# Layer 3 of a four-layer convolution kernel: shifted copies replaced by 64x64 products that share the array with Layer 0's mixing

## The chip, the cores and the metric

The kernel runs on one core of one Trainium2 chip. The metric is the device time of one execution in microseconds; the time before is the median of three executions. One execution was also recorded by the hardware profiler, and all rows and waits below come from that record.

## The reference

The input is x of shape (16, 64, 128, 128): 16 images of 64 channels, float32. Four layers are added to it in turn, each on a group-normalized input `_gn` (32 groups of two channels):

```python
# layer 0: gram matrix of the channels, then a 64x64 matrix
y = einsum('bcd,bdn->bcn', einsum('bcn,bdn->bcd', xf, xf) / N, xf);  x = x + einsum('oc,bchw->bohw', conv_w, y)
# layer 1: 3x3 Scharr filters per channel
x = x + abs(conv(gn, kx)) + abs(conv(gn, ky))
# layer 2: quarter of the channels moved a column left, a quarter right, then a dense 3x3 convolution
x = x + conv3x3(shift(gn), W) + b
# layer 3: dense 3x3 convolution with weights -1, 0, 1, a 1x1 convolution, batch normalization, clip
y = conv1x1(conv3x3(gn, w_bin), w1x1) + b1x1
x = x + clip(leaky((y - mean) * rsqrt(var + EPS) * gamma + beta), 0, 255)
```

Layer 3's mean and variance run over all images, so its output can be finished only when all 16 images have passed its convolution.

## The kernel before, in words

**Staging.** Each image is cut into NS = 8 pieces of 8 rows per half image (128 partitions hold 64 channels twice). The loop at line 1059 runs over steps; in a step each stage works on one piece: `Front` (Layers 0 and 1) starts image b at step 15 + 8b, `Layer2` ten steps later, `Layer3` ten more (line 1009). So Layer 3 runs in steps 35 to 162, 128 pieces. `Front` mixes its last piece at step 140, `Layer2` ends at step 152, and Layer 3 is alone for the last ten steps. After that a last stage reads y and x3 back, applies the batch normalization and writes the output.

**Order.** Every instruction keeps its program order on its engine (`InOrder`, line 63). A step has four quarters, q = 0 to 3, and in each the stages come in the order Layer3, Layer2, Front (line 1067). What follows on an engine in a quarter is thus written out by hand.

**Layers 2 and 3 as products.** A pair of output rows shares work: `one` is the sum over the tap row that both need (`shared`, line 750), and `two` has the two rows' own parts, from row differences `d2` or `d3` that VectorE makes (`difference`, line 706). All products are 128 contracted rows by 64 output channels, issued two at a time, one for each half of the array's columns (`issue`, line 730; leftovers wait in `held` until `issue_rest` before Front in q = 1 and 3). Of the weights of `own` (line 753), one output half is dense, that is, it takes both input halves: three taps, three products. The other half is sparse: only one of the two 64-row input halves counts, so that a plain tap would use half of the array's rows:

```python
TO_PAIRS = [(0, 0, 0, 1), (0, 0, 1, 0), (0, 1, 0, 0), (1, 0, 1, 2), (1, 1, 0, 2), (1, 1, 1, 1)]   # n, input half, output half, ky
def single(table, n):        # the output half of n that is sparse, and its only input half
```

For n = 0 that is input half 0 to output half 1, for n = 1 input half 1 to output half 0. Before, two of the sparse half's three taps are packed into one product with full rows: `pk` holds both taps' weights, and a twin tile `qd` holds the difference and, in the other 64 partitions, a copy moved by a column. The third tap is a product of its own. So `own` has 3 + 2 products for each of n = 0, 1, and with the 3 + 3 of `shared` Layer 3 has 16 per piece, eight pairs; Layer 2 has the same 16.

**The twins.** Layer 2's are made by two DMAs on the GpSimd queue each (line 810). Layer 3's are made by ScalarE: `twin` at line 952 issues two copies of 64x512; `twin(0)` in q = 3, `twin(1)` in q = 0 of the next step (lines 999 and 963). `own(n=0)` of Layer 3 is issued in q = 0, `own(n=1)` in q = 1.

**Mixing.** Layer 0's product is `abd` (64x64 per half) times x. For the first three images it is issued as a pair of 128x64 products (`mix`, line 589). From image 3 on, `mix_four` (line 579) issues four 64x64 products in q = 1, one on each of the array's four 64x64 blocks. For that, `load` (line 564) lays x out so that one half of the partitions has the first four rows of the piece in both image halves, and the other half the last four: row block g then produces `po` of group g in both column blocks. Its outputs are two PSUM tiles, `po` and `g`, each with one buffer, which ScalarE reads into `xh`.

**Around them in a step.** VectorE makes the Scharr sums `u`, `e` (eight passes over 128x1024), then `y` = `two` + `c` for Layer 3 in q = 2 (line 990), `d3[0]` in q = 2 (line 996), `d3[1]` in q = 3 (line 1000), `d2[1]` at the end of q = 3, and `x3` and `d2[0]` in q = 0. ScalarE reads `po` into `xh`, normalizes, takes absolute values and squares, and copies `one` to `c`. In three steps out of eight, until about 1590 us, TensorE also has 42 or 44 gram products. At an image's end a chain of tiny operations (`coefficients`, line 288) crosses VectorE, TensorE and ScalarE; its first link, `s`, waits on VectorE for a square that ScalarE makes.

Of the kernel before, what the change touches and what calls it, by code (L numbers as in the profile page):

```python
# [10 lines left out]
F32 = mybir.dt.float32  # L11
# [5 lines left out]
P = 128  # L17
# [3 lines left out]
R = 8  # L21
NS = HH // R
EARLY = 3
CP = 4
# [84 lines left out]
def tile_kernel(ctx: ExitStack, tc: tile.TileContext, x, cw_h, w2_t, b2, wbin_t, w1_t, b1, gamma, beta, consts, out):  # L109
# [56 lines left out]
    def cols(o):  # L166
        return slice(o * C, (o + 1) * C)
# [51 lines left out]
    for name in ("d2", "d3"):  # L219
        diffs[name] = wpool.tile([P, 2, CP, W + 2], F32, name=name)  # L220
        pool.memset(diffs[name], 0.0)
        twins[name] = wpool.tile([P, 2, CP, W + 2], F32, name=f"q{name}")
        pool.memset(twins[name], 0.0)

    def weights_of_layer_3(ky):

# [11 lines left out]
    def other_weights():  # L238
        for n in range(2):
            o = 1 - single(TO_SLOTS, n)[0]  # L240
            pool.tensor_copy(wm[:, :, cols(o)], w2[:, n, :, cols(o)])

        for name, w, table in (("pk2", w2, TO_SLOTS), ("pk3", w3, TO_PAIRS)):
            dve.tensor_add(w[:, 2], w[:, 0], w[:, 1])
            packed[name] = wpool.tile([P, 2, C], F32, name=name)
            for n in range(2):
                o, i = single(table, n)
                for kx, half in ((1, i), (0, 1 - i)):
                    pool.tensor_copy(
                        packed[name][half * C:(half + 1) * C, n], w[i * C:(i + 1) * C, n, kx, o * C:(o + 1) * C]  # L250
                    )
# [297 lines left out]
    class Front:  # L549
# [14 lines left out]
        def load(self, i):  # L564
            b = self.b
            t = xin.tile([P, R, W], F32, tag="x", name=f"x_{b}_{i}")
            if self.four:

                t = t.rearrange("p (h r) w -> p h r w", h=2)
                v = x[b].rearrange("c (h r) w -> c h (r w)", h=2)  # L570
                for g in range(2):
                    j = (i * R + g * CP) * W
                    sp.dma_start(t[cols(g)].rearrange("p h r w -> p h (r w)"), v[:, :, j:j + CP * W])
            else:
                for h in range(2):
                    sp.dma_start(flat(t[h * C:(h + 1) * C]), halves(x[b].rearrange("c h w -> (c h w)"), h, i * R, R))
            self.xs[i] = t

        def mix_four(self, i):

            for g, (pool, tag) in enumerate(((ps_po, "po"), (ps_g, "g"))):
                self.po[i, g] = pool.tile([P, CP, W], F32, tag=tag, name=f"po_{self.b}_{i}_{g}")
            t = self.xs.pop(i)
            order = 1 - last[0], last[0]
            for g in range(2):
                for h in order:
                    pe.matmul(self.po[i, g][cols(h)], self.abd[cols(g), cols(g)], t[cols(g), h], start=True, stop=True)

        def mix(self, i, g):
            if self.b == 0 and (i, g) in ((0, 1), (1, 0)):  # L590
# [15 lines left out]
        def at(self, i, q):  # L606
            b = self.b
            if q == 0:
                if i == -3:

                    self.xe = xin.tile([P, W], F32, tag="xe", name=f"xe_{b}", bufs=1)
                    sp.dma_start(self.xe[lo], x[b][:, HH, :])
                    sp.dma_start(self.xe[hi], x[b][:, HH - 1, :])
                    sp.dma_start(x2_d[b][0:W].rearrange("(p w) -> p w", p=1), w0[0:1, 0:W])
                if i + 3 < NS and i + 3 not in self.xs:
                    self.load(i + 3)
                if -1 <= i < NS - 1:
                    self.prepare(i + 1, 1)
                if 1 <= i:
                    self.store(i - 1)  # L620
                    act.activation(
                        junk.rearrange("p (j w) -> p j w", w=W), self.x2.pop(i - 1), AF.Square,
                        accum_out=self.st[:, 1, i - 1:i],
                    )
                if i == NS:
                    chains.append(coefficients(self.st, lambda co: coefs2.update({b: co}), b2_sb))
            if q == 1 and -2 <= i < NS - 2:
                if i == -2:
                    self.abd, self.co = lead.pop(b)
                if i == -2 and not self.four:  # L630
                    self.pe = ps_g.tile([P, CP, W], F32, tag="g", name=f"pe_{b}")[:, 0, :]
                    small_product(self.pe, self.abd, self.xe)
                if self.four:
                    self.mix_four(i + 2)
                else:
                    self.mix(i + 2, 0)
            if q == 3 and i == -2 and self.four:
                self.pe = ps_po.tile([P, CP, W], F32, tag="po", name=f"pe_{b}")[:, 0, :]
                small_product(self.pe, self.abd, self.xe)
            if (i, q) == ((-1, 0) if self.four else (-2, 2)):  # L640
                nc.gpsimd.memset(self.chunk(0)[lo, 0, :], 0.0)
                self.normalized(self.chunk(0)[hi, 0, 1:1 + W], self.pe[hi], hi)
                self.pel = small.tile([P, W], F32, tag="pel", name=f"pel_{b}", bufs=1)
                self.normalized(self.pel[lo], self.pe[lo], lo)
            if q == 2:
                if i == NS - 2:
                    nc.gpsimd.memset(self.chunk(NS - 1)[hi, R + 1, :], 0.0)
                    act.copy(self.chunk(NS - 1)[lo, R + 1, 1:1 + W], self.pel[lo])
            if 0 <= i < NS:
                self.sobel(i, q)  # L650
            if q == 2 and -2 <= i < NS - 2:
                self.prepare(i + 2, 0)
            if q == 3 and -2 <= i < NS - 2 and not self.four:
                self.mix(i + 2, 1)
                self.xs.pop(i + 2)
# [85 lines left out]
    def issue_rest():  # L741
        while held[0] or held[1]:
            emit(1 - last[0] if held[1 - last[0]] else last[0])

    def products(p, wts, srcs):
        issue([taps(o, p, wts, srcs) for o in range(2)])

# [5 lines left out]
    def own(p, n, table, wt, name, m=CP, both=None):  # L753
# [7 lines left out]
        ]  # L761
        issue(some)


    tiles3 = {}

# [157 lines left out]
    class Layer3:  # L924
# [24 lines left out]
                norm(t[:, CP + 1:R, :], tiles[i][:, 1, 0:CP - 1], self.co)  # L949
                norm(t[:, R, :], tiles[i][:, 1, CP - 1, :], self.edge["upper"])  # L950

        def twin(self, n):

            d, q = diffs["d3"], twins["d3"]
            _, i = single(TO_PAIRS, n)
            act.copy(q[cols(i), n, :, 1:1 + W], d[cols(i), n, :, 1:1 + W])
            act.copy(q[cols(1 - i), n, :, 2:2 + W], d[cols(i), n, :, 1:1 + W])

        def at(self, i, q):
            b = self.b  # L960
            n = b * NS + i
            if q == 0 and 0 <= i < NS:
                self.twin(1)
                t = self.v[i]
                one = ps_one.tile([P, CP, W], F32, tag="one", name=f"one3_{b}_{i}")
                two = ps_two.tile([P, 2, CP, W], F32, tag="two", name=f"two3_{b}_{i}")
                self.p[i] = two, one
                shared(one, w3[:, 2], t)
                own(two[:, 0], 0, TO_PAIRS, w3, "d3")
            if q == 1:  # L970
                if 0 <= i < NS:
                    two, one = self.p[i]
                    own(two[:, 1], 1, TO_PAIRS, w3, "d3")
                    self.v.pop(i)
                    self.c = ring.tile([P, CP * W], F32, tag="c3", name=f"c3_{b}_{i}", bufs=1)
                    act.activation(self.c, flat(one), AF.Identity, bias=b1_sb)
                if i + 1 < NS:
                    self.prepare(i + 1)
                if 1 <= i:
                    y = self.y.pop(i - 1)  # L980
                    for s in range(2):
                        for z in range(2):
                            v = pairs(y_d[b], s)[:, (i - 1) * R:i * R, :].rearrange("c (n z) w -> c z n w", z=2)
                            sp.dma_start(v[:, z], y[s * C:(s + 1) * C, z])
# [11 lines left out]
                    difference("d3", 0, self.v[i + 1])  # L996
            if q == 3:
                if i + 1 < NS:
                    self.twin(0)
                    difference("d3", 1, self.v[i + 1])  # L1000
                if 0 <= i < NS:
                    act.activation(
                        junk, self.y[i].rearrange("p s j w -> p (s j w)"), AF.Square,
                        accum_out=bn_sq[:, n:n + 1],
                    )
# [53 lines left out]
    for step in range(starts[2][1] - 2, steps):  # L1059
        now[0] = step  # L1060
        for q in range(4):
# [5 lines left out]
            for stage, at in starts:  # L1067
                if stage is Front and q in (1, 3):
                    issue_rest()
                for b in range(B):  # L1070
                    run(stage, b, step - at - NS * b, q)
            if q in (0, 3):
                for b in range(B):
                    run(Layer2, b, step - starts[1][1] - NS * b, f"last of {q}")
# [116 lines left out]
```

## Time and profile before

| what | value |
|---|---|
| median of three executions | 2729.09 us (2726.27 to 2729.88) |
| span of the profiled execution | 2727.2 us, first to last instruction |
| TensorE, products | 2162.2 us busy, 79% of the span |
| VectorE | 2170.0 us busy, 80% |
| ScalarE | 2079.2 us busy, 76% |
| GpSimd | 852.7 us busy, 31% |
| ScalarE's copies into `qd` | 512, 315.4 us, 616 ns each |
| mixing products on 64x64 blocks | 832 records |
| last stage (from 2300 us) | DMA-bound: TensorE idle, 414 GB/s |

Each product of float32 is two records in the trace, one per pass; a pair of products is therefore four records. "us" in a timeline row is the time from the first start to the last end of the records merged in it, and the end of a product is modelled, so rows that follow each other overlap a little. Spacing is read from start to start. The number in brackets is the time for which the engine was idle before the row, with what ended it. The span lies 1.9 us under the median of the timed executions and inside their range; of the profiled execution no other time than its span is given.

### The profile page before, as it was taken

To read this page: it belongs to the slowest core of one execution; us is meant where nothing else is said; L and a number is where in the kernel's file an instruction comes from. 1 tells how busy PE (TensorE), PEld (TensorE's weight loads), DVE (VectorE), ACT (ScalarE), POOL (GpSimd) and SP (SyncE) were. 2 spreads that over 40 slices of the span, in tenths; PEclk is the share of its full clock that TensorE was granted. 3 is DMA by queue.
4 is the path that set the end of the run, shared out by engine and by line. 5 is a ranking of instruction groups with operands and counts; after the bars stand their busy time and mean duration, and the time that the engine had idled before them with its cause. 6 is when DMAs were issued, how large, how long until landed. Compare 5 with 4: busy or idle time off the path is not lost. (4 is left out here: it accounts for less than half of the span.)

```text
span 2727.2 us, 45742 instructions
## 1 busy us (share of the span) xinstructions
PE 2162.2 (79%) x14804; PEld 913.7 (34%) x14804; DVE 2170.0 (80%) x3495; ACT 2079.2 (76%) x3065; POOL 852.7 (31%) x1350
## 2 busy tenths in 40 slices
PE   6578899999999999999999999999999993000000
PEld 4234433434343434343434343333334641000000
DVE  4999999899999999999999999999995335333332
ACT  4766889898989898989898989899997667333332
POOL 2045424443434243333343334445453200000000
PEclk8689999999999999999999999999999996555555
DMA  8799878888888888888888887888877868999999
GB/s 199 205 239 239 226 197 239 225 235 225 235 228 237 227 226 229 226 227 234 225 224 237 214 204 203 207 211 216 224 200 186 226 188 314 420 420 420 420 420 385
DMA packets 693598, 685.93 MB, mean 252 GB/s; under 512 B 60096, under 2 KB 580448, under 8 KB 693360
## 3 DMA queue, kind: packets, MB, share of 16 engines
q1 hardware_dynamic: 668208, 613.83, 76.4%
q0 software_dynamic: 25152, 69.18, 10.0%
q8 instruction: 119, 1.95, 0.3%
q14 instruction: 119, 0.97, 0.1%
HBM read 346.23 MB, written 268.44 MB: 225 GB/s over the span
## 5 line engine op out<-in xcount | busy, mean ns | idle before, releaser
L73 PE MATMUL two<-d,w 128*64 128x508 f32 (+2 forms) x2560 | 848.9, 587 | 0.0
L73 PE MATMUL two<-d,wi 128*64 128x508 f32 (+3 forms) x1536 | 573.8, 577 | 0.0
L73 PE MATMUL two<-qd,pk 128*64 128x512 f32 (+1 forms) x1024 | 520.0, 589 | 24.5 <-DMA qd<-d 16.6
L73 POOL DMA_DIRECT2D qd<-d x512 | 271.1, 532 | 852.8 <-DVE d L73 323.9
L73 POOL TENSOR_SCALAR edges<-v,co 64x8 f32<-64x8 f32 x512 | 340.2, 664 | 349.0 <-ACT v L73 216.8
L73 DVE TENSOR_TENSOR d<-v 128x512 f32<-128x512 f32 (+1 forms) x512 | 346.6, 680 | 65.3 <-issue 37.5
L73 PEld LDWEIGHTS two<-d,w 128*64 128x64 f32 x2560 | 278.7, 136 | 320.0 <-issue 270.9
L73 PE MATMUL one<-v,w 128*64 128x508 f32 (+2 forms) x1600 | 364.3, 579 | 1.1 <-ACT v L73 1.1
L73 PE MATMUL one<-v,wi 128*64 128x508 f32 (+3 forms) x1536 | 353.3, 591 | 2.0 <-issue 1.4
L73 ACT COPY qd<-d 64x512 f32<-64x512 f32 x512 | 315.4, 616 | 19.9 <-DVE d L73 13.8
L73 DVE SCALAR_TENSOR_TENSOR e<-e 128x1032 f32<-128x1032 f32 (+1 forms) x256 | 313.0, 1223 | 0.0
L73 ACT ACTIVATE xh<-po,co 128x128 f32<-128x128 f32 (+1 forms) x480 | 275.9, 624 | 23.9 <-PE po L73 21.4
L73 PEld LDWEIGHTS two<-d,wi 128*64 128x64 f32 x1536 | 178.0, 135 | 197.4 <-issue 180.0
L73 DVE SCALAR_TENSOR_TENSOR y<-two,c 128x1024 f32<-128x1024 f32 x128 | 156.0, 1219 | 97.8 <-ACT v L73 45.6
L73 POOL TENSOR_SCALAR v<-v,kc 128x9 f32<-128x9 f32 x256 | 213.4, 847 | 12.0
L73 PE MATMUL po<-x,abd 64*64 64x512 f32 (+1 forms) x1024 | 177.1, 640 | 45.6 <-ACT xh L73 42.2
L73 ACT ACTIVATE v<-x,co 128x1024 f32<-128x1024 f32 (+3 forms) x256 | 203.8, 847 | 0.0
L73 ACT ACTIVATE u<-u 128x1024 f32<-128x1024 f32 x128 | 135.5, 1059 | 75.6 <-DVE u L73 74.6
L73 PEld LDWEIGHTS two<-qd,pk 128*64 128x64 f32 x1024 | 131.6, 135 | 176.9 <-issue 85.5
L73 PEld LDWEIGHTS one<-v,w 128*64 128x64 f32 x1600 | 130.9, 136 | 175.3 <-issue 146.5
L73 ACT ACTIVATE c<-one,co 128x512 f32<-128x512 f32 x128 | 86.7, 678 | 127.4 <-PE one L73 124.0
L73 DVE SCALAR_TENSOR_TENSOR u<-xh 128x1170 f32<-128x1170 f32 x128 | 175.4, 1370 | 4.2 <-ACT xh L73 4.1
(165 smaller groups left out, 3325.2 us busy)
## 6 DMA issues: line engine op xcount, KB each, us to landing
x<-in_x SPq DMA_DIRECT2D x256, 256.0 KB, 4.6
x_d<-u SPq DMA_DIRECT2D x512, 128.0 KB, 4.0
y_d<-y SPq DMA_DIRECT2D x512, 128.0 KB, 3.8
x_d<-x SPq DMA_DIRECT2D x496, 128.0 KB, 2.7
xr<-in_x SPq DMA_DIRECT2D x120, 512.0 KB, 5.9
qd<-d POOLq DMA_DIRECT2D x256, 130.0 KB, 3.3
qd<-d POOLq DMA_DIRECT2D x256, 129.8 KB, 3.8
v<-x_d SPq DMA_DIRECT2D x448, 72.1 KB, 3.0
```

What stands on the lines that cost most here:

```text
L73: return self.tc.keep_in_program_order(call(*args, **kwargs))
```

## The change

The shifted copies of Layer 3 go: `twin`, its two calls, the tile `qd3` and the packed weights `pk3`. `dense` issues the two dense halves of `two` together in q = 0: three taps for each half, six products of 128x64. `sparse` in q = 1 makes the three taps of each sparse half as 64x64 products on their own row and column block (row block 0 to column block 1, and row block 1 to column block 0), in a queue `blocks[0]`. `mix_four` no longer issues: it puts its four products, now each on row block h and column block h, in pairs in `blocks[1]`. `issue_blocks` takes one pair of each queue in turn: sparse, mixing, sparse, mixing, sparse. It is called from Front in q = 1 after `issue_rest`, and once more after the stages for steps without mixing. `load` is the same for all images now: 64 partitions by 4 KB in each of its two DMAs, where before a DMA of the later images had two runs of 2 KB for each partition.

```diff
-        twins[name] = wpool.tile([P, 2, CP, W + 2], F32, name=f"q{name}")
-        pool.memset(twins[name], 0.0)
+    twins["d2"] = wpool.tile([P, 2, CP, W + 2], F32, name="qd2")
+    pool.memset(twins["d2"], 0.0)
...
             dve.tensor_add(w[:, 2], w[:, 0], w[:, 1])
+            if name == "pk3":
+                continue
             packed[name] = wpool.tile([P, 2, C], F32, name=name)
...
-            if self.four:
-
-                t = t.rearrange("p (h r) w -> p h r w", h=2)
-                v = x[b].rearrange("c (h r) w -> c h (r w)", h=2)
-                for g in range(2):
-                    j = (i * R + g * CP) * W
-                    sp.dma_start(t[cols(g)].rearrange("p h r w -> p h (r w)"), v[:, :, j:j + CP * W])
-            else:
-                for h in range(2):
-                    sp.dma_start(flat(t[h * C:(h + 1) * C]), halves(x[b].rearrange("c h w -> (c h w)"), h, i * R, R))
+            for h in range(2):
+                sp.dma_start(flat(t[h * C:(h + 1) * C]), halves(x[b].rearrange("c h w -> (c h w)"), h, i * R, R))
...
-            order = 1 - last[0], last[0]
             for g in range(2):
-                for h in order:
-                    pe.matmul(self.po[i, g][cols(h)], self.abd[cols(g), cols(g)], t[cols(g), h], start=True, stop=True)
+                rows = slice(g * CP, (g + 1) * CP)
+                blocks[1].append([
+                    (self.po[i, g][cols(h)], self.abd[cols(h), cols(h)], t[cols(h), rows, :], True, True) for h in range(2)
+                ])
...
                 if self.four:
                     self.mix_four(i + 2)
+                    issue_blocks()
...
+    blocks = deque(), deque()
+
+    def issue_blocks():
+
+        while blocks[0] or blocks[1]:
+            for made in blocks:
+                for dst, wt, src, start, stop in (made.popleft() if made else ()):
+                    pe.matmul(dst, wt, src, start=start, stop=stop)
+        last[0] = 1
...
+    def dense(two, table, wt, name):
+
+        some = [None, None]
+        for n in range(2):
+            o, _ = single(table, n)
+            some[1 - o] = taps(1 - o, two[:, n], [wt[:, n]], [diffs[name][:, n]], 1)
+        issue(some)
+
+    def sparse(two, table, wt, name):
+
+        made = []
+        for n in range(2):
+            o, i = single(table, n)
+            made.append([
+                (dst, w[cols(i)], src[cols(i)]) for dst, w, src in taps(o, two[:, n], [wt[:, n]], [diffs[name][:, n]], 1)
+            ])
+        for m, both in enumerate(zip(*made)):
+            blocks[0].append([a + (m == 0, m == 2) for a in both])
...
-        def twin(self, n):
-
-            d, q = diffs["d3"], twins["d3"]
-            _, i = single(TO_PAIRS, n)
-            act.copy(q[cols(i), n, :, 1:1 + W], d[cols(i), n, :, 1:1 + W])
-            act.copy(q[cols(1 - i), n, :, 2:2 + W], d[cols(i), n, :, 1:1 + W])
-
...
             if q == 0 and 0 <= i < NS:
-                self.twin(1)
...
-                own(two[:, 0], 0, TO_PAIRS, w3, "d3")
+                dense(two, TO_PAIRS, w3, "d3")
...
-                    own(two[:, 1], 1, TO_PAIRS, w3, "d3")
+                    sparse(two, TO_PAIRS, w3, "d3")
...
                 if i + 1 < NS:
-                    self.twin(0)
                     difference("d3", 1, self.v[i + 1])
...
                 for b in range(B):
                     run(stage, b, step - at - NS * b, q)
+            issue_blocks()
```

## The prediction

> **What bounds the kernel now.** I read the page's busy times and groups first, then the table of busy time by stretch, then TensorE's timeline step by step, and last ScalarE's and VectorE's beside it.
>
> ```profile
> PE 2162.2 (79%) x14804; PEld 913.7 (34%) x14804; DVE 2170.0 (80%) x3495; ACT 2079.2 (76%) x3065; POOL 852.7 (31%) x1350
> L73 ACT COPY qd<-d 64x512 f32<-64x512 f32 x512 | 315.4, 616 | 19.9 <-DVE d L73 13.8
> ```
>
> Three engines look equally busy, and the change takes the copies' 315.4 us, the second row, from ScalarE. Whether that is worth anything depends on the stage (columns: stretch, length, then busy us of PE, PEld, DVE, ACT, POOL, clock, DMA):
>
> ```profile
> 600.00:2030.00 1430.00, 1417.60 (x9320) 558.89 (x9318) 1370.66 (x2229) 1291.88 (x1991) 570.96 (x909) 1.00 0.85 222
> 2030.00:2195.00 165.00, 165.00 (x839) 91.01 (x837) 85.48 (x155) 113.46 (x175) 56.14 (x115) 1.00 0.77 204
> 2195.00:2275.00 80.00, 77.89 (x351) 32.19 (x347) 25.14 (x51) 57.01 (x93) 0.00 (x0) 1.00 0.65 195
> ```
>
> While all stages run, TensorE is idle for 12.4 of 1430 us. Once mixing has ended (2030 to 2195) it is never idle. So only TensorE's own order and spacing count. A Layer 3 piece where nothing waits, and one that waits:
>
> ```profile
> 1253.66 2.73 PE L73 MATMUL one<-v,w 128*64 128x512 f32 x12
> ...
> 1260.60 1.09 PE L73 MATMUL po<-x,abd 64*64 64x512 f32 x8
> ```
>
> ```profile
> 1237.53 2.75 PE L73 MATMUL one<-v,w 128*64 128x512 f32 x12
> ...
> 1241.33 0.64 PE L73 MATMUL two<-qd,pk 128*64 128x512 f32 x1 [0.22 <-ACT qd L73]
> ...
> 1245.75 1.09 PE L73 MATMUL po<-x,abd 64*64 64x512 f32 x8
> ```
>
> From the first product of the piece to the mixing it is 6.94 us in one and 8.22 in the other. The bracket shows only 0.22: while one column half waits for its twin the other goes on, so that the engine counts as busy. ScalarE and VectorE in the slow piece:
>
> ```profile
> 1240.03 1.24 ACT L73 COPY qd<-d 64x512 f32<-64x512 f32 x2
> 1241.30 1.23 ACT L73 COPY xw<-xr 128x1024 f32<-128x1024 f32 x1
> 1242.54 1.25 ACT L73 COPY qd<-d 64x512 f32<-64x512 f32 x2
> ```
>
> ```profile
> 1213.43 0.17 DVE L73 TENSOR_REDUCE s<-st 128x2 f32<-128x16 f32 x1 [2.11 <-ACT junk L73]
> ...
> 1236.44 0.70 DVE L73 TENSOR_TENSOR d<-v 128x512 f32<-128x512 f32 x1
> ...
> 1238.29 0.68 DVE L73 TENSOR_TENSOR d<-v 128x512 f32<-128x512 f32 x1
> ```
>
> VectorE has both differences at 1238.97, in time for the 1240.09 at which the piece first needs one; ScalarE, late in its queue, has the twins at 1241.27 and 1243.79.
>
> **What the skill says.** The Trainium skill, TensorEngine Tiling (Array Packing), section Key Properties, says that changing the tiling mode, not just the tile, drains TensorE. The trace agrees. A step of Layers 2 and 3 without mixing:
>
> ```profile
> 2127.40 2.98 PE L73 MATMUL one<-v,w 128*64 128x512 f32 x12
> ...
> 2141.09 0.85 PE L73 MATMUL one<-v,w 128*64 128x512 f32 x2
> ```
>
> It is 13.69 us for 16 pairs, 0.855 a pair. A step with mixing and no wait is 14.85 (the `one` of Layer 3 begins at 1895.32 and again at 1910.17). The mixing thus costs 1.16: a slot of 0.855 and 0.31 for going to 64x64 blocks and back. I go by the 0.31. The same page, Gotcha 1: PSUM Pressure, says that different row tiles cannot use one PSUM bank at once. Before, each row block of the mixing has a bank of its own; after, both write the same one, in different partitions. No row shows that case; it is a rival below.
>
> **The change part by part.**
>
> *Slots in a full step.* Before: Layer 2 has 8 slots, Layer 3 has 8, the mixing 1, and one trip to 64x64 blocks. After: Layer 2 has 8, Layer 3's `shared` 3, `dense` 3, and the block phase 3, with the four mixing products inside its first two slots; one trip. 17 slots and 0.31 both times: 14.85. For all 104 pieces with four-block mixing (13 images of 8) the product time is unchanged. Bounds for the new kind of slot: in the mixing the two passes start 0.480 apart, against 0.427 within a run of pairs, but so do the first two after the return (0.484), so I take 0.427 for later passes; 0.480 for all is the upper end. Nothing in the trace points below 0.427, since a pass streams the same 512 columns.
>
> *Pieces without mixing.* 24 pieces: steps 35 and 36 (image 2 still mixes in pairs), 141 to 152 with Layer 2, 153 to 162 alone. Each pays a slot and a trip: 1.16. For the first 14, TensorE is the bound: +16.3. Alone, a piece now takes 7.82 and waits for ScalarE, because the twins stand between `d3` and the products:
>
> ```profile
> 2228.04 1.22 DVE L73 SCALAR_TENSOR_TENSOR y<-two,c 128x1024 f32<-128x1024 f32 x1 [5.38 <-issue]
> 2229.19 0.08 DVE L73 DVE_READ_ACCUMULATOR y<-two,c 128x1 f32 x1
> 2229.19 1.29 DVE L73 TENSOR_TENSOR d<-v 128x512 f32<-128x512 f32 x2
> ```
>
> After, 9 slots and the trip are 8.0. Another loop is as long: the end of `sparse`, `y` and both differences (2.44), `dense` (2.56), `sparse` with its drain (3.0), about 8.1. So 0.3 for each of ten: +3.
>
> *Waits on Layer 3's twins.* They go. I took the time from the piece's first product to the mixing, less 6.93, for each piece from 415 to 2016 us: two late pieces per image, 1.2 us each in the middle images, less in the last three, 21.5 us in all. What is late next? `dense` needs `d3[1]` 2.56 after the piece begins; in all these pieces it ends at 2.11 or earlier. TensorE would then come earlier to Layer 2, whose `d2[0]` twins are DMAs and land about 4.9 us after VectorE's difference; it already waits 11 us for them in all. VectorE does not wait for TensorE there, so these waits would absorb the gain if VectorE stayed where it is. It does not: at an image's end `s` waits 2.11 for a square that ScalarE makes behind two twins; without them ScalarE comes about 1.4 earlier, and VectorE keeps that until the gram steps. I let 2 of 21.5 come back: -19.5.
>
> *At nothing.* The mixing is issued two slots earlier and its second pair needs `g` read by ScalarE: that ends at 7.41 in the slow piece, 4.9 without 2.5 us of twins, and is needed at about 6. `y` on VectorE, and behind it `d3[0]`, comes after `sparse`, 1.2 later than after `own`; in steps with gram products VectorE has that room, elsewhere it is 2 to 5 us behind. If that cover is gone, VectorE's 14.33 us of work a step sets the pace, still under 14.85. x arrives a step ahead, and its two DMAs on SP stay two, of the same 256 KB. GpSimd loses a memset and four small copies early, and SP nothing; no DMA of Layer 3 was on their queues.
>
> *Sum* against the profiled span of 2727.2: -19.5 + 16.3 + 3 = -0.2. The median stands 1.9 above that span, so 2729.
>
> **The rivals.**
> 1. Slower: passes on the blocks stay 0.480 apart, since four weights are loaded for each. Four more passes (six, less the two already counted) times 128 pieces times 0.053: +27, 2756. It decides the sign from 0.01 us a pass. For: the mixing's row. Against: the pair after the trip starts just so, and the eight loads of the mixing lie within 0.21 us.
> 2. Slower: the waits return at `d2[0]`'s DMA, because VectorE is as late as before. Only 5 of 21.5 are won: +14, 2743. For: the 11 us. Against: the wait of `s`.
> 3. Faster: the earlier VectorE also takes away those 11 us: 2718.
> 4. The change doesn't do what it says: the four blocks do not run side by side, because of the shared bank. Then the mixing is four products in a row against three slots, 0.85 times 104: +89, 2818. The mixing's old form ran four at once, but with two banks.
>
> **How the numbers follow.** Forecast 0.36 (2723.6 to 2734.5, that is, within the 0.2% which a measurement of this kernel can tell from no change), rival 1 0.20, rival 2 0.20, rival 3 0.20, rival 4 0.04. Faster is rival 3; slower is rivals 1, 2 and 4. The range goes from rival 3 with both waits fully gone (-32.5 + 19.3, 2716) to just past rival 1, 2758; rival 4 is left out.
>
> **What would show it.** Steps without mixing at 14.85 instead of 13.68 and the last pieces near 8.1; passes in the block phase 0.427 apart, four starting within 0.03 us (rivals 1 and 4); Layer 3 pieces all near 8.0 from first product to Layer 2's; waits of `two` on the `qd` DMA at 8 to 12 us (rivals 2 and 3); ScalarE 315 us less busy; `s` waiting under 1 us. The forecast is wrong if the waits at `d2[0]` grow as Layer 3's vanish, or if a block slot is not 0.855.

## The result and the profile after

| | median, us | range | runs |
|---|---|---|---|
| before | 2729.5 | 2726.3 to 2730.9 | 4 |
| after | 2741.8 | 2738.6 to 2745.2 | 4 |

The ratio is 1.0049, 95% interval 1.0035 to 1.0063: slower by more than 0.2%, where no change was forecast. The profiled run of after took 2738.6, the lowest of its four; its span is 2736.8, against 2727.2 before. So the medians differ by 12.3 and the two traced spans by 9.6; the account below is of the 9.6. The granted clock is 1.00 in both from 600 to 2030 us.

The page of after, lines of engines and groups:

```profile
PE 2167.4 (79%) x15316; PEld 865.4 (32%) x15316; DVE 2169.2 (79%) x3495; ACT 1769.4 (65%) x2553; POOL 927.1 (34%) x1345
...
L73 PE MATMUL two<-qd,pk 128*64 128x512 f32 (+1 forms) x512 | 257.1, 583 | 26.3 <-DMA qd<-d 26.3
```

ScalarE is 310 us less busy and TensorE 5 us busier. The second row is now Layer 2's alone. What TensorE waited for in the stretch in which all stages run, first before, then after (columns: us in total, times, longest):

```profile
PE two L73 <- DMA qd<-d: 8.3, 12, 1.3
PE two L73 <- ACT qd L73: 7.0, 13, 0.7
```

```profile
PE two L73 <- DMA qd<-d: 17.6, 13, 2.8
PE one L73 <- issue: 1.7, 2, 1.4
```

The wait for ScalarE has gone; the one for `d2[0]`'s twin DMA has doubled, in about as many places. Most of it (15.8 of after's 17.6 us) lies at an image's end, in the step of Layer 3's last piece of that image, called the late step from here on. TensorE's timeline of after, in one late step:

```profile
1216.88 2.73 PE L73 MATMUL one<-v,w 128*64 128x512 f32 x12
1219.44 3.31 PE L73 MATMUL two<-d,w 128*64 128x512 f32 x14
1222.12 0.65 PE L73 MATMUL po<-x,abd 64*64 64x512 f32 x2
1222.59 0.59 PE L73 MATMUL two<-d,w 64*64 64x512 f32 x2
1222.60 0.60 PE L73 MATMUL po<-x,abd 64*64 64x512 f32 x2
1223.02 0.59 PE L73 MATMUL two<-d,w 64*64 64x508 f32 x2
...
1224.82 2.80 PE L73 MATMUL one<-v,wi 128*64 128x512 f32 x12
...
1231.52 0.61 PE L73 MATMUL two<-qd,pk 128*64 128x512 f32 x1 [1.34 <-DMA qd<-d]
```

Layer 3's piece takes 7.94 us (1216.88 to 1224.82), with no wait in it. Two mixing and two sparse products start within 0.02 us of each other, later passes 0.43 apart, though both row blocks of the mixing write one bank. Then, in Layer 2, TensorE stops for the twin.

A step with neither mixing nor waits, and two of the last pieces, from the same timeline:

```profile
2110.77 2.73 PE L73 MATMUL one<-v,w 128*64 128x512 f32 x12
2113.33 5.44 PE L73 MATMUL two<-d,w 128*64 128x512 f32 x24
...
2125.60 2.73 PE L73 MATMUL one<-v,w 128*64 128x512 f32 x12
...
2225.13 2.78 PE L73 MATMUL one<-v,w 128*64 128x512 f32 x12
2233.21 2.78 PE L73 MATMUL one<-v,w 128*64 128x512 f32 x12
```

The first takes 14.83 us where it was 13.69, the last piece 8.08 where it was 7.82. For the account I took each of the 128 pieces of Layer 3 from its first product to Layer 2's first (L3), and from there to the next piece (L2). Sums in us:

| | before | after | difference |
|---|---|---|---|
| start of the first piece | 312.5 | 309.6 | -2.9 |
| steps 35 and 36, L3 and L2 | 39.4 | 41.8 | +2.4 |
| 104 pieces with four-block mixing, L3 | 935.3 | 912.2 | -23.1 |
| the same, L2 | 743.7 | 757.2 | +13.5 |
| 12 steps without mixing, L3 and L2 | 165.4 | 179.5 | +14.1 |
| nine intervals of Layer 3 alone | 70.5 | 73.4 | +2.9 |
| TensorE's last product to the end | 448.8 | 451.8 | +2.9 |

With the last piece (0.1 shorter) and rounding this is the +9.6 of the spans. The start lies anywhere from 310 to 318 in the versions below, most of which do nothing there. The last row is 448.8 to 449.6 in every version whose last ten pieces have the old form; with the new form it is 451.3 to 451.8 in six and 449.0 to 450.7 in three, and what decides it was not found.

Row four is the one that the forecast had at +2. Nearly all of it (13.4) stands in the 13 late steps, 7.6 in two of them, at 429.7 and 692.2 us. And 13.0 stand in the nine late steps of the images beside which xr, the copy of x for a later image's gram, is still fetched; in the four after that, L2 of the late steps is 29.8 us before and 30.2 after.

### The profile page after: what moved, and what is told of

It is laid out like the page before. It is cut to its first block, busy times and chain, and to the rows that moved or that the text cites. A ratio compares the mean times of both kernels' runs of the same rounds, so it can differ in the third digit from the quotient of the medians.

```text
span 2736.8 us, 46307 instructions
## 1 busy us (share of the span) xinstructions
PE 2167.4 (79%) x15316; PEld 865.4 (32%) x15316; DVE 2169.2 (79%) x3495; ACT 1769.4 (65%) x2553; POOL 927.1 (34%) x1345
## 4 chain that ended last, share of the span: by engine, by line
PE 69%; DMA 19%; DVE 5%; issue 2%; SPq 2%; ACT 1%; POOL 0%; DVEq 0%; POOLq 0%; ACTq 0%
PE two L73 41%; PE one L73 22%; PE bank L73 4%; DMA qd<-d 2%; DVE u L73 2%; DMA end_x<-x_d 2%; DMA out<-end_x 2%; SPq L73 2%; DVE e L73 2%; DMA end_x<-y_d 1%; DMA out<-xw 1%; DMA xw<-x_d 1%; DMA xw<-y_d 1%; PE pg L73 1%; DMA v<-x_d 1%
## 5 line engine op out<-in xcount | busy, mean ns | idle before, releaser
L73 PE MATMUL two<-d,w 128*64 128x508 f32 (+4 forms) x3584 | 958.5, 590 | 0.0
L73 PE MATMUL two<-d,wi 128*64 128x508 f32 (+3 forms) x1536 | 575.7, 580 | 0.0
L73 POOL DMA_DIRECT2D qd<-d x512 | 271.0, 531 | 899.3 <-DVE d L73 368.1
L73 POOL TENSOR_SCALAR edges<-v,co 64x8 f32<-64x8 f32 x512 | 414.4, 809 | 229.2 <-ACT v L73 144.2
L73 PEld LDWEIGHTS two<-d,w 128*64 128x64 f32 (+1 forms) x3584 | 292.8, 134 | 514.5 <-issue 493.6
L73 DVE TENSOR_TENSOR d<-v 128x512 f32<-128x512 f32 (+1 forms) x512 | 346.9, 680 | 73.2 <-issue 45.7
L73 PE MATMUL one<-v,w 128*64 128x508 f32 (+2 forms) x1600 | 361.1, 579 | 0.0
L73 PE MATMUL one<-v,wi 128*64 128x508 f32 (+3 forms) x1536 | 349.1, 588 | 2.1 <-issue 1.7
L73 DVE SCALAR_TENSOR_TENSOR e<-e 128x1032 f32<-128x1032 f32 (+1 forms) x256 | 313.1, 1223 | 0.0
L73 PE MATMUL po<-x,abd 64*64 64x512 f32 (+1 forms) x1024 | 265.0, 629 | 46.6 <-ACT xh L73 43.6
L73 ACT ACTIVATE xh<-po,co 128x128 f32<-128x128 f32 (+1 forms) x480 | 275.5, 625 | 26.1 <-PE po L73 19.7
L73 PE MATMUL two<-qd,pk 128*64 128x512 f32 (+1 forms) x512 | 257.1, 583 | 26.3 <-DMA qd<-d 26.3
L73 ACT ACTIVATE u<-u 128x1024 f32<-128x1024 f32 x128 | 135.7, 1060 | 206.3 <-DVE u L73 206.2
L73 DVE SCALAR_TENSOR_TENSOR y<-two,c 128x1024 f32<-128x1024 f32 x128 | 156.0, 1219 | 114.3 <-issue 99.9
L73 PEld LDWEIGHTS two<-d,wi 128*64 128x64 f32 x1536 | 176.9, 136 | 205.1 <-issue 189.8
L73 POOL TENSOR_SCALAR v<-v,kc 128x9 f32<-128x9 f32 x256 | 216.8, 860 | 12.0
L73 ACT ACTIVATE v<-x,co 128x1024 f32<-128x1024 f32 (+3 forms) x256 | 203.9, 847 | 0.0
L73 ACT ACTIVATE c<-one,co 128x512 f32<-128x512 f32 x128 | 86.7, 677 | 159.7 <-PE one L73 155.1
L73 PEld LDWEIGHTS one<-v,w 128*64 128x64 f32 x1600 | 122.9, 137 | 183.2 <-issue 171.8
L73 ACT ACTIVATE v<-v,co 128x1154 f32<-128x1154 f32 x128 | 172.2, 1345 | 11.0 <-DMA v<-x_d 6.3
L73 DVE SCALAR_TENSOR_TENSOR u<-xh 128x1170 f32<-128x1170 f32 x128 | 175.4, 1370 | 3.9 <-ACT xh L73 3.8
L73 DVE SCALAR_TENSOR_TENSOR u<-xh,co,u 128x1024 f32<-128x1024 f32 x128 | 163.7, 1279 | 1.1 <-ACT u L73 1.1
```

The costliest lines, as they stand in the source:

```text
L73: return self.tc.keep_in_program_order(call(*args, **kwargs))
```

## The experiments

Theories on row four: A, x now goes in 4-KB packets, which hold up the twins; B, it is what stands ahead of the twins on the DMA queues at that moment; C, the twins cannot land earlier whatever is done. Unless said otherwise an edit is made on after, and waits are those of `two` on the `qd` DMA, 400 to 2040 us. Ratios are to the kernel before, with their 95% intervals. The code shown is the main part of each edit.

**1. The old form where nothing mixes.** In 24 pieces (`n < 2 or n >= 106`):

```
+                if n < 2 or n >= 106:
+                    own(two[:, 0], 0, TO_PAIRS, w3, "d3")
+                else:
                     dense(two, TO_PAIRS, w3, "d3")
```

and likewise for `sparse` and the copies.

> After, but the 24 pieces of Layer 3 beside which nothing mixes on four blocks keep the old form: the shifted copies on ScalarE and 2.5 slots each way instead of dense and sparse. If a piece without mixing pays a slot and a trip (1.16 us, 14 times) and 0.3 us in each of the last ten, the 12 steps without mixing go back from 14.84 to 13.68, the last pieces from 8.08 to 7.8, and the time falls by 16 to 19, to 2723 to 2726, under both kernels. If the added 12.3 us of the change lie elsewhere (other waits take over in these steps), it falls by under 8.

Measured: 2716.2, ratio 0.9944 (0.9933 to 0.9956). The steps without mixing in its timeline:

```profile
2085.87 2.98 PE L73 MATMUL one<-v,w 128*64 128x512 f32 x12
2099.55 2.98 PE L73 MATMUL one<-v,w 128*64 128x512 f32 x12
```

13.68 again, and 70.5 for the last nine intervals. The rows for these 24 pieces and the last row give 2.3 + 14.0 + 2.9 + 2.4 = 21.6 back, of 23.4 between the two spans. L2 of the 104 pieces, which this edit doesn't touch, is 6.3 shorter (750.9), and the start is 4.0 later. In the six late steps from 820 to 1480 us xr is issued 2.4 to 5.4 us ahead of the twins here and 1.5 to 4.1 in after; experiment 6 shows what that means. So the time falls by more than the 16 to 19 expected, but the price of an empty slot and a trip stands.

**2. The load of ScalarE alone.** The four copies are still made, but nothing reads them:

```
+                self.twin(1)
                 t = self.v[i]
...
+                    self.twin(0)
                     difference("d3", 1, self.v[i + 1])
```

> After, but ScalarE still makes the four shifted copies of every piece of Layer 3, into a buffer that no product reads: the change's products with the old load of ScalarE. If the earlier VectorE (s waits 0.67 in place of 2.11) is worth something after the change, it is lost here: d2[0] ends at 9.4 us in the late steps again, TensorE waits up to 1.3 us more in each image, and the time rises by 10 to 18, to 2752 to 2760. If the moment of d2[0] on VectorE does not matter because its twins land late whatever it does, the time stays within 4 us of 2742. In no case do TensorE's waits for Layer 3's twins come back.

Measured: 2748.5, ratio 1.0064 (1.0052 to 1.0076), +6.7 over after: between the two expectations. VectorE is as late as the first says; its `s` and `d2[0]` in the late step:

```profile
1217.34 0.17 DVE L73 TENSOR_REDUCE s<-st 128x2 f32<-128x16 f32 x1 [2.05 <-ACT junk L73]
...
1234.03 0.69 DVE L73 TENSOR_TENSOR d<-v 128x512 f32<-128x512 f32 x1
```

That is 2.05 against after's 0.67, and `d2[0]` ends 9.46 after the step begins (1225.26) against 8.07. The 104 pieces take 927.3 (L3) and 749.8 (L2), in sum 1677.1; before had 1679.0, after 1669.4. So 7.7 of the 9.6 that the 104 pieces win are lost again when ScalarE's queue is as long as before, though TensorE is free of the twins: Layer 3's mixing then waits for ScalarE instead (`[0.26 <-ACT xh L73]` ahead of the second pair, in the piece at 1225.26).

**3. The packets of x.** First with two fetches of 128 partitions, then with the same two fetches as after and a gap in the tile:

```
+                v = x[b].rearrange("c (h r) w -> h c r w", h=2)
+                for g in range(2):
+                    rows = slice(i * R + g * CP, i * R + (g + 1) * CP)
+                    sp.dma_start(flat(t[:, g * CP:(g + 1) * CP]), v[:, :, rows, :].rearrange("h c r w -> h c (r w)"))
```

```
+                t = xin.tile([P, 2, CP * W + 4], F32, tag="x", name=f"x_{b}_{i}")
...
+                    sp.dma_start(t[cols(h), :, 0:CP * W], v.rearrange("c (g n) -> c g n", g=2))
```

> After, but x of an image with four-block mixing is fetched in two DMAs of 128 partitions by 2 KB in place of two of 64 partitions by 4 KB; same bytes, same place on SP. Theory A (the twins of d2[0] land late because the 4-KB packets of x stand ahead of them on the DMA engines): TensorE's waits of two on the qd DMA fall from 17.6 us to 8 or less between 400 and 2040 us, and the time falls by about 10 to 15, to 2727 to 2733. Theory B (it is the moment at which SP issues x, 0.4 to 1.5 us ahead of the twins where it was 3.3 us before): the waits stay within 2 us of 17.6 and the time stays within 4 of the changed kernel's 2742. Theory C (the twin cannot land before a fixed moment of SP's saturated queue): as B.

> After, but the tile of x has a gap of 16 bytes between its two column groups, so that the same two fetches of 64 partitions go in packets of 2 KB (two per partition) instead of 4 KB; everything else as after. In the earlier try at this, x took 13.6 us to land, because its fetch had an outer dimension of 2; here the outer dimension is 64 as in the two kernels. Theory A (4-KB packets of x hold up the twins of d2[0]): TensorE's waits of two on the qd DMA fall from 17.6 us to 8 or less between 400 and 2040 us, time 2727 to 2733. Theory B (the moment of x on SP): waits within 3 us of 17.6, time within 4 of 2742.

Measured: the first took 3561.0 (ratio 1.304): no test of A, since the fetch itself became slow (last section). The second took 2740.8 (1.0043, 1.0030 to 1.0056), with waits of 18.6 us. A is false.

**4. x elsewhere.** Issued one quarter later; by ScalarE; or two quarters earlier (the old place is closed where the place is new):

```
+            if q == 1 and self.four and i + 3 < NS:
+                self.load(i + 3)
```

```
+            eng = act if self.four else sp
             for h in range(2):
-                sp.dma_start(
+                eng.dma_start(
```

```
+            if q == 2 and self.four and i + 4 < NS:
+                self.load(i + 4)
```

> After, but x for a later step is issued on SP one quarter later, behind Layer 3's stores and Layer 2's load of that quarter, so that it no longer stands just ahead of the twins of d2[0]; it still has more than half a step until the mixing reads it. Theory B (the moment of x on the queues): TensorE's waits of two on the qd DMA fall from 17.6 to under 9 us and the time by 8 to 15. Theory A (the size of its packets): about the same, since those packets are out of the way too. Theory C (the twins cannot land earlier whatever is ahead of them): waits of 16 to 19 us and no change in time. New waits of po for x would show that the later place is too late.

> After, but the two fetches of x per step of an image with four-block mixing are issued by ScalarE instead of SP. SP's queue, which is without a gap around the late steps, gets two issues a step shorter, so everything behind x on it comes 1.2 to 2.8 us earlier, and x stands elsewhere among the transfers. Theory B (moment of x): waits of two on the qd DMA fall to under 9 us, time 2727 to 2735. Theory C (the twin cannot land earlier): 2738 to 2745. ScalarE's two issues cost it at most 1.2 us a step, of the 2.5 that the change has taken from it; if that is felt, s waits over 1 us again.

> After, but x is issued on SP two quarters earlier, behind the stores of x3 of the step before (its buffer has been free since that step's mixing), so that it is neither next to xr nor just ahead of the twins of d2[0] in the steps after an image's end. Theory B (x and xr, 768 KB, go ahead of the twins on the same DMA engines): waits of two on the qd DMA fall from 17.6 to 4 to 9 us, without the waits for x that the later place brought, and the time falls to 2727 to 2734. If xr alone is enough to hold the twins, waits stay above 12 and the time above 2737.

Measured: later 2757.9 (1.0096), by ScalarE 2770.6 (1.0149), earlier 2741.1 (1.0037). The waits of the later place:

```profile
PE po L73 <- DMA x<-in_x: 9.0, 15, 1.9
PE two L73 <- DMA qd<-d: 4.2, 5, 1.7
```

The twins come in time more often, but x doesn't: L3 of the 104 pieces grows from 912.2 to 943.7. This speaks for B, but weakly, since TensorE is also later.

By ScalarE, the waits stay (15.5), where B expected under 9, and ScalarE waits 158.4 us for Layer 2's v, which was 3.7; why v comes late was not followed up. Yet in the ten late steps that still wait, the twins are used 3.6 to 4.4 us after their issue, sooner than in after (5.9 to 6.0 in four middle images). They wait because the twins are issued 9.5 to 11.0 us after the step begins, which was 8.6 in the middle images of after. So this run is no evidence against B.

The earlier place changed nothing (waits 17.7), but it was no test: between the old place of x in these steps and the new one lies only xr. x and xr had changed places and stayed neighbours.

**5. The twin earlier.** `d2[0]` and its two transfers ahead of the making of x3, on after, with edit 1, and on before:

```
+                if 0 <= i < NS:
+                    difference("d2", 0, self.v[i], m)
+                    self.twin(0)
                 if 1 <= i:
                     two = self.p.pop(i - 1)[0]
...
-                if 0 <= i < NS:
-                    difference("d2", 0, self.v[i], m)
-                    self.twin(0)
```

> After, but in each step of Layer 2 the difference d2[0] and its two twin transfers are issued ahead of the edges' add and the making of x3, in place of behind them: d2[0] ends about 1.8 us earlier on VectorE (6.2 instead of 8.07 after Layer 3's first product in the late steps), the twins are issued as much earlier. If the forecast failed because those twins land late, the waits of two on the qd DMA go from 17.6 to under 4 us and the time falls by 12 to 17, to 2725 to 2730. If the twins' transfers are held by what the DMA engines do at that time, the waits fall by less than half and the time stays above 2734. What is late next: x3 is 0.7 us later, and with it the two of Layer 2 comes free later; not before it is needed at 10.5.

> The two edits together: the old form of Layer 3 in the 24 pieces without four-block mixing, and d2[0] with its twins ahead of x3. If the two parts are independent, the gains add: 2716 less 8 to 13, that is 2703 to 2709. If the waits at d2[0] are already small in the first (13.2 us in its trace), the second gives less, 2709 to 2714.

> The kernel before, with d2[0] and its twins ahead of x3, as in the run of after that went to 2731.9. It gives the size of the change where the wait at d2[0] is out of the way on both sides. If the kernel before only waits at d2[0] because TensorE is not held by Layer 3's twins there, its 8.3 us of waits on the qd DMA fall below 4 and it ends at 2722 to 2726; the change then costs 6 to 10 with this wait gone too, and the forecast's sum (-0.2) is off by more than this wait. If it does not gain (2727 to 2731), the wait at d2[0] is the whole difference between the forecast and the result.

Measured: on after 2731.9 (1.0009, 1.0000 to 1.0017), waits 7.0; with edit 1 2711.5 (0.9936, 0.9924 to 0.9949), waits 12.7; on before 2728.3 (0.9996, 0.9988 to 1.0004). On after it wins 10. With edit 1 it wins less, about 5: the twins are issued 1.65 earlier (6.98 after the step begins) and yet TensorE gets them at 14.4 to 15.1 in five middle images, as late as in after (14.6 to 15.1). Their place beside xr tells the two versions apart. In the six late steps from 820 to 1480 us, on after, the twins go out ahead of the xr of that moment in five, and TensorE then waits 0.12 us at most for them; in the sixth they go out 0.07 us behind it, and TensorE waits 1.35. With edit 1 they go out 0.4 to 1.6 us behind xr in all six, and TensorE waits 0.7 to 1.8 in each. The kernel before wins nothing: its L2 falls from 743.7 to 738.8 and its L3 rises from 935.3 to 939.7.

**6. xr.** Five of an image's eight fetches of xr (512 KB each) are moved to the end of a later quarter, most by two, on after and with the other edits:

```
-                if m + 3 < NS:
-                    self.load(m + 3)
+            m = {13: 3, 14: 4, 17: 5, 21: 6, 25: 7}.get(4 * i + q)
+            if m is not None:
+                self.load(m)
```

> After, but the five later fetches of xr of an image (512 KB each, for the gram) are issued on SP two quarters later, behind Layer 2's load of v, instead of just ahead of x and of the twins of d2[0]. If xr is what holds the twins, the waits of two on the qd DMA fall from 17.6 us to under 8 and the time to 2726 to 2733. If it does not matter what stands ahead of the twins (the DMA engines are simply that busy, with what comes behind taking xr's place), the waits stay at 14 to 20 and the time at 2738 to 2745.

> The kernel before with xr two quarters later. Before, the twins of d2[0] waited for VectorE more than for xr (8.3 us of waits, transfers of 3.3 to 4.4 us after the second issue), and Layer 3's twin copies set the rest: at most 3 us won, 2726 to 2731. Then the change and the xr edit belong together, and xr's place is the reason for the added 12. If before falls as far as the changed kernel did (to 2719 to 2723), xr's place costs both the same and the change itself has a loss of 10 that the forecast missed elsewhere.

Measured: 2731.4 (1.0001, 0.9993 to 1.0009), waits 7.8, L2 of the 104 pieces 744.8; before 2729.3 (0.9999, 0.9991 to 1.0008). The queues in the same late step. SP's and GpSimd's timelines of after:

```profile
1223.35 0.54 SPq L73 DMA_DIRECT2D xr<-in_x  x1
1223.98 1.17 SPq L73 DMA_DIRECT2D x<-in_x  x2
```

```profile
1225.50 1.03 POOL L73 DMA_DIRECT2D qd<-d  x2 [4.87 <-PE two L73]
```

Of before:

```profile
1226.33 0.39 SPq L73 DMA_DIRECT2D xr<-in_x  x1
1226.82 1.29 SPq L73 DMA_DIRECT2D x<-in_x  x2
```

```profile
1231.37 1.03 POOL L73 DMA_DIRECT2D qd<-d  x2 [4.87 <-PE po L73]
```

With xr later, and TensorE's first product with the twin behind it:

```profile
1213.71 0.39 SPq L73 DMA_DIRECT2D xr<-in_x  x1
1214.20 4.54 SPq L73 DMA_DIRECT2D x_d<-x  x5
1218.83 1.18 SPq L73 DMA_DIRECT2D x<-in_x  x2
```

```profile
1221.17 1.03 POOL L73 DMA_DIRECT2D qd<-d  x2 [4.87 <-PE two L73]
```

```profile
1225.67 0.59 PE L73 MATMUL two<-qd,pk 128*64 128x512 f32 x1
```

Before, the twins go out 5.0 us behind xr and are used 4.42 after that (1235.79). After, they go out 2.15 behind it, with x between, and are used 6.02 later (1231.52). With xr 7.46 ahead they are there within 4.50, without a wait, although x still stands just ahead. So it is xr and x together, 768 KB, in the 2.2 us ahead of the twins; with either moved away (4, later; 6) the waits fall from 17.6 to 4.2 and 7.8. The other images agree: in the nine late steps with an xr it stands 4.0 to 5.3 us ahead of the twins before, 1.0 to 4.1 after and 4.2 to 8.0 with xr later. That is B, shown on the changed kernel; C is false. The Trainium skill, DMA: Bandwidth & Descriptors, section Rules for kernel authors, says that transfers from SP, ScalarE and GpSimd run on the same 16 engines and interleave; in this step that costs 1.6 us or more (6.02 against 4.42, where nothing waited).

**7. The versions that beat both.** Edits 1 and 5 with x earlier; with xr later; with both; and 5 and 6 on before, as their counterpart:

> The old form of Layer 3 where nothing mixes on four blocks, d2[0] with its twins ahead of x3, and x two quarters earlier. In the version with the first two edits (2711.5) 12.7 us of waits for the twins were left, though they were issued 1.65 earlier: they landed at 14.4 to 14.6 after Layer 3's first product all the same, so the transfers ahead of them held them. If those are x, the waits go under 4 and the time is 2700 to 2706; if they are xr alone, it stays at 2708 to 2713.

> The old form of Layer 3 where nothing mixes on four blocks, d2[0] with its twins ahead of x3 (2711.5 so far, 12.7 us of waits for the twins left), and xr two quarters later. If xr holds the twins: waits under 4 us, 2700 to 2705. If not: 2709 to 2713.

> The same with x two quarters earlier too (2705.1 and 3.1 us of waits without xr's move). There is little left to win: 2702 to 2706 in either case; a time above 2708 would say that xr's later place costs something itself.

> The kernel before with both queue edits, d2[0] and its twins ahead of x3, and xr two quarters later: the counterpart of the version at 2703.6, which has the new form of Layer 3 wherever mixing fills the blocks. Layer 3's waits for its copies (21.5 us) stay, so 2723 to 2729; the new form in 104 pieces is then worth 20 to 25 us.

| | time, us | ratio to before | waits | L3, L2 of the 104 pieces |
|---|---|---|---|---|
| 1, 5, x earlier | 2705.1 | 0.9911 (0.9897 to 0.9924) | 3.1 | 912.5, 742.2 |
| 1, 5, xr later | 2703.6 | 0.9898 (0.9885 to 0.9912) | 0.6 | 912.4, 740.6 |
| all four | 2702.9 | 0.9895 (0.9880 to 0.9910) | 1.6 | 912.4, 740.9 |
| before, with 5 and xr later | 2728.5 | 0.9990 (0.9981 to 0.9998) | | 944.8, 733.7 |

The last row is the key to the kernel before. With either queue edit or both, L3 and L2 sum to 1678.5 (1679.0 untouched): what L2 wins, L3 pays. The trace of before with xr later shows why, in the piece behind the late step (VectorE, ScalarE, TensorE):

```profile
1237.29 0.68 DVE L73 TENSOR_TENSOR d<-v 128x512 f32<-128x512 f32 x1
```

```profile
1239.04 1.24 ACT L73 COPY qd<-d 64x512 f32<-64x512 f32 x2
...
1241.54 1.24 ACT L73 COPY qd<-d 64x512 f32<-64x512 f32 x2
```

```profile
1236.42 2.73 PE L73 MATMUL one<-v,w 128*64 128x512 f32 x12
...
1240.34 0.64 PE L73 MATMUL two<-qd,pk 128*64 128x512 f32 x1 [0.34 <-ACT qd L73]
```

Both differences are there at 1237.97, but ScalarE, whose timeline shows no gap from 1221.86 to 1249, gets to its copies at 1239.04 and 1241.54. TensorE, now early, waits for them. With the new form the queue edits count in full, 1669.4 to 1653.0. The new form in the 104 pieces, with old in the rest, is thus worth 25 us, once the transfers are out of its way.

## Why the prediction was wrong

- **Slots in a full step: right.** A step with mixing and without waits is 14.84; in the step shown block passes are 0.425 to 0.429 apart from the second on. Rivals 1 and 4 are out. The Trainium skill's row-tile rule (TensorEngine Tiling (Array Packing), Gotcha 1: PSUM Pressure) was rightly kept to a rival: two row blocks writing different partitions of one bank cost nothing measurable here.
- **Pieces without mixing: right.** +16.3 and +3 forecast; 2.4 + 14.1 = 16.5 and 2.9 measured, and edit 1 takes them back. The 2.9 behind the last product was not forecast, and neither were the 2.9 won ahead of the first piece.
- **Waits on Layer 3's twins: gone as forecast.** 21.5 forecast, 23.1 measured in L3 of the 104 pieces.
- **"I let 2 of 21.5 come back": the step that failed.** 13.5 came back, at `d2[0]`'s twins, as rival 2 has it by place; its price (16.5 come back, 2743) is close too. But the reason in rival 2, a late VectorE, is not what happened. VectorE came 1.4 earlier, as the forecast says: `s` waited 0.67, `d2[0]` ended 8.07 after the step began instead of 9.45, and the twins were issued at 8.6 instead of 10.0. After's `s` and `d2[0]`, and the `d2[0]` of before:

```profile
1207.57 0.17 DVE L73 TENSOR_REDUCE s<-st 128x2 f32<-128x16 f32 x1 [0.67 <-ACT junk L73]
...
1224.26 0.69 DVE L73 TENSOR_TENSOR d<-v 128x512 f32<-128x512 f32 x1
```

```profile
1230.13 0.69 DVE L73 TENSOR_TENSOR d<-v 128x512 f32<-128x512 f32 x1
```

- **"land about 4.9 us after VectorE's difference": the figure in it that did not hold.** It was taken as fixed. From the end of `d2[0]` to the use of its twin it is 4.97 before (1230.82 to 1235.79) and 6.57 after (1224.95 to 1231.52), which eats the 1.4 and more.
- **"x arrives a step ahead, and its two DMAs on SP stay two", "SP nothing": the line that hid it.** Nothing was added to SP, but two things moved against each other. The twins are issued 1.4 earlier in the step, and xr is issued 1.5 later in it (6.47 after the step begins instead of 4.93), since TensorE's step comes 4.5 us earlier in the run and that xr only 3.0. Together they bring the twins from 5.0 to 2.15 behind xr. Before, SP still stood idle for 1.55 ahead of that xr; after, it issues from 1212 to 1231 with gaps of 0.11 us or less, so it could not move along. The forecast asked whether VectorE comes earlier, and not what its transfer then lands among.
- **The rest of the sum stands.** With xr out of the way after takes 2731.4, and with `d2[0]` first 2731.9, against 2729.0 forecast; L2 is then 744.8 and 747.3, so that 1.1 and 3.6 come back, about the 2 of the forecast. Rival 3 is out as well: even then 7.8 and 7.0 us of waits for the twins are left, where before had 8.3.

## What to carry to other kernels

When a change lets an engine run earlier, place its next transfer anew among the transfers of the queues that don't move: the same twin took 4.4 us from issue to use with 768 KB issued in the 5.0 us ahead of it, and 6.0 with the same 768 KB in the 2.2 us ahead. Where a wait shrinks in one place and grows in another by as much (1679.0, 1678.5, 1678.5, 1678.5 before), look for another engine's queue that sets the pace; here experiment 2 and the ScalarE rows of experiment 7 point to ScalarE's. And a form that fills empty array blocks pays only where there is something to fill them: otherwise it costs 1.16 us a step here, so that keeping both forms in one kernel is worth it (experiment 1).

## What the runs showed of the hardware

- Two fetches of x with an outer dimension of 2 (2 x 64 x 2 KB) cost 820 us in all against the same bytes with 64 outermost. In the trace 256 packets of 97 ns of one step's fetch were spread over 13.9 us, 1.8 at a time (from 1542 us), where after's 128 packets of 272 ns took 3.2 us, 11 at a time (from 1227 us). The Trainium skill, DMA: Bandwidth & Descriptors, section Rules for kernel authors, states the rule: an outermost dimension of c under 16 confines a transfer to at most c engines. The 1.8 agree with it. SP is held up behind these fetches: there the next four stores of y take 8.59 us to issue, against 2.63 to 4.31 in after's steps around the late one. TensorE's wait for x over that kernel, from its page:

```profile
L73 PE MATMUL po<-x,abd 64*64 64x512 f32 (+1 forms) x1024 | 332.5, 735 | 423.7 <-DMA x<-in_x 296.7
```

- Packets of 4 KB or 2 KB for x made no difference that the runs can show (2741.8 and 2740.8).
